# Routing's steps on VectorE with an operand in PSUM, prefix sums by scans, |q| from the bank, and a new order, in an attention and mixture-of-experts layer

## The chip, the cores and the metric

The kernel runs on one NeuronCore of a Trainium2 chip. The metric is the device time of one execution in microseconds (us), as the median of several. TensorE is called PE in the profile (PEld is its weight loads), VectorE is DVE, ScalarE ACT, GpSimd POOL, and SyncE, which issues most DMAs, SP.

## What is computed

The input is x, 4 sequences of 1024 tokens with 128 channels. It is normalised, and two branches are added to x:

```python
xn = layernorm(x)
out = x + attention(xn) + experts(xn)

# attention: 16 heads of 8 channels
q, k, v = heads(xn @ W_attn + b_attn)
s = q @ k.T;  s = s - s.mean(-1)
s = s / (abs(s).mean(-1) + 1e-6) * score_gain        # over all keys
r = max(where(causal, s, -1000), 0) ** 4
y = (r / (r.sum(-1) + 1e-6)) @ v;  return y @ W_proj + b_proj

# experts: 8 experts, each token goes to its best 2
logits = xn @ gate_w + gate_b
topv, topi = top_k(logits, 2);  probs = softmax(topv)
for e in range(8):
    h = (xn @ w1[e] + b1[e]) * (xn @ w2[e] + b2[e])
    y = silu(h @ wg[e] + bg[e]) @ w3[e] + b3[e]
    out += sum(probs * (topi == e)) * y
```

All arithmetic is in float32.

## The kernel before

**The order is a planner's.** The kernel first records nodes: each has a name, a cost for each engine that may do it, what it depends on, the buffers it takes and gives back, and a rank. `Plan.run` then goes through them as a list scheduler: of the nodes that are ready, it takes the one with the earliest start by its own costs, less a bonus `SOONER` for the name (and the name with an engine), and, where starts are equal, the lowest rank plus `RANK` for the name. So two tables of numbers and the costs decide both the order and which engine does a step that can go to more than one (relu on ScalarE or VectorE, squares on ScalarE or GpSimd, sums of |s| on VectorE or ScalarE). The order on each engine is then fixed in the program: every engine works through its own list, strictly in order, and waits by semaphores for the others.

**Start** (to about 35 us). Four `norm` calls make normalised tokens in `blk` buffers (130 columns a token: 128 channels, a column for a gate's weight, a column for a row number), transpose them (`xT`), and compute the gate's logits into `lg` (L529). `prepare(0)` makes keys, queries and values of the first sequence: k and q matmuls (L794), evacuations from the PSUM bank on ScalarE (L802, L806), |q| by ScalarE from the evacuated q (L832), a tiny constant added to it on VectorE (L836), a matmul with the mean |k| (L855) that bounds |s|, and a scaling of q by a power of two that comes from the bound's exponent bits (L841, L844). `blocks` (L885 to L890) forms running sums of k over blocks of 128 keys, and `heads` (L926, L932) uses them. For the other sequences this is done later, between attention work.

**Routing** (`route`) is the mixture's bookkeeping, with the token on the partition and 32 blocks of 128 tokens by 8 experts, 256 elements, on the free axis. All its scratch lies in three SBUF buffers of kind `u`:

- `top` (L586 to L594) finds the best and the second expert by max, compare, multiply by a preference and compare again, and writes two 0/1 arrays `hot` and their sum.
- `counts` (L604, L605) multiplies that sum by a triangle of ones and by ones, so that each token gets its rank within its block and each block its totals.
- `places` (L613 to L619) makes prefix sums over the 32 blocks by six doubling steps of a copy and an add. `tiles_of` (L627 to L644) counts how many tiles of 256 slots each expert needs and sums these over the experts by three doubling steps.
- `slots_of` (L650 to L658), once for each of the two choices, gives each token the row in the scatter buffer `xs`. `owners` (L663 to L671) says which expert each of the 39 tiles belongs to; `bias` (L683) gathers the biases of the tiles' experts by six matmuls.
- `weights` (L700 to L709) makes the two softmax weights from an exp on ScalarE (L599) and fills `we`, which is needed for the bias b3 in the output projection.

Then 64 indirect DMAs on GpSimd's queue scatter 128 rows each to `xs` (L747), each after the one before has landed. The rows' weight column is set to the first weight by `weights` (L704) and to the second by GpSimd (L732) before the second half.

**Attention** is worked in eight chunks (four sequences, two halves of 512 queries), and each chunk in four groups of four heads. `up` (L971) computes all scores of a query block for the sum of |s|, which VectorE (L984) or ScalarE (L986) takes from the bank. `score` (L1095) computes the causal ones transposed; a mask with max (VectorE, L1114) and relu (ScalarE L1121 or VectorE L1123) bring them to SBUF buffers `u1`, two squarings (ScalarE L1146 or GpSimd L1148) to buffers `u`, and `av` (L1171, with L1162 for the sum of the relus) multiplies by the values. Transposes (L1039), a normalisation on VectorE and ScalarE (L1048 to L1060), and the output projection (L1212 to L1237) end a chunk.

**Experts** run beside attention from 290 us on: 39 tiles of 256 slots. For each, SP loads the rows and the expert's weights, PE transposes and does three matrix products (L1276, L1286, L1293, L1302), and GpSimd adds the rows to a DRAM accumulator `acc` by two indirect DMAs (`give`, L1322). At the end `collect` reloads the accumulator in four DMAs (L1410), adds it to the output (L1419), and eight DMAs store it (L1424).

Of the kernel before, what the change touches and what calls it, by code (L numbers as in the profile page):

```python
# [9 lines left out]
I32 = mybir.dt.int32  # L10
U32 = mybir.dt.uint32
AF = mybir.ActivationFunctionType
ALU = mybir.AluOpType
# [3 lines left out]
P = 128  # L17
# [34 lines left out]
class Plan:  # L52
# [6 lines left out]
    SOONER = {"score": 0.67, "mask": -0.22, "norm": -0.9, "tbias": -0.55, "count": 0.79, "rows": 0.11, "v": -0.28, "top": 1.05, "wT": 0.08, "kappa": 0.16, "gateT": 0.62, "k": 0.33, "abs": -0.58, "ys": 0.25, "stats": -0.21, "exp": -0.3, "sq": -0.97, "bound": 0.23, "proj": -0.33, "scale": -0.84, "least": 1.02, "xg": 0.24, "give": 0.78, "bias": 0.7, "yT": -0.13, "std": 0.01, "turn": 0.11, "sum": -0.3, "sums": -0.07, "heads": -0.18, "gate": -0.46, "headsT": -0.01, "normal": -0.04, "load": -0.33, "second": -0.2, "h": 0.16, "relu": -0.23, "keys": -0.53, "y@DVE": -1.2, "gate@DVE": -0.05, "relu@DVE": -0.49, "xT": 0.31, "q@DVE": -0.03, "xg@DVE": -0.53, "yT@ACT": -0.29, "relu@ACT": -0.03, "abs@ACT": 0.05, "out": -1.18, "yT@DVE": 0.3, "xT@DVE": -0.72, "norm@DVE": 0.4, "place": -0.51, "gate@ACT": 0.54, "g": 0.1, "wT@ACT": -0.22, "y@ACT": -0.99, "heads@DVE": -0.21, "fill": 0.06, "heads@ACT": 0.29, "mean": 0.04, "y": 0.98, "abs@DVE": 0.31, "ys@DVE": -0.24, "sq@ACT": 0.32, "warm": 0.42, "xg@ACT": -0.73, "norm@ACT": 0.74, "up": 0.2, "q": 0.22}  # L59
    RANK = {"score": 14, "proj": -177, "yT": 11, "k": -27, "xg": -79, "sums": -3, "h": 8, "sq": 29, "reload": 126, "tbias": -22, "normal": -23, "bound": 51, "top": -177, "headsT": 9, "weight": 88, "spill": -20, "blocks": 6, "place": -4, "sum": -25, "kappa": -91, "std": 28, "gateT": -159, "count": 17, "scatter": 175, "xT": -7, "heads": 20, "y": 3, "exp": -5, "second": -240, "load": 6, "relu": 124, "keys": -42, "mask": -227, "rows": -24, "scale": 209, "out": 16, "turn": -13, "wT": 13, "fill": 16, "ys": -33, "av": -7, "bias": 7, "gain": -11, "g": 186, "q": -113, "give": -27, "gate": -124, "absq": 32, "norm": 26, "warm": 17}  # L60
# [105 lines left out]
def layer_kernel(  # L166
# [152 lines left out]
    for i in range(kinds["V"][0]):  # L319
# [9 lines left out]
    ahead = keep([P, P], "ahead")  # L329
    nc.gpsimd.memset(ahead, 1.0)  # L330
    nc.gpsimd.affine_select(
        out=ahead, in_=ahead, compare_op=ALU.is_gt, fill=0.0,
        base=0, pattern=[[1, P]], channel_multiplier=-1,
# [4 lines left out]
    steps = keep([P, NT // TS], "steps")  # L338
    tiles_f = keep([P, N_TILES], "tiles_f")
    expert_f = keep([P, 1], "expert_f")  # L340
    for t, pattern, base, cm in (
        (first, [[-1, E]], E, 0), (steps, [[TS, NT // TS]], 0, 0),
        (tiles_f, [[1, N_TILES]], 0, 0), (expert_f, [[0, 1]], 0, 1),
    ):
        nc.gpsimd.iota(t, pattern=pattern, base=base, channel_multiplier=cm, allow_small_or_imprecise_dtypes=True)
# [70 lines left out]
    slot = [keep([P, NTB], f"slot_{k}", I32) for k in range(2)]  # L416
    whole = [keep([P, NTB], f"whole_{k}", I32) for k in range(2)]
    owner = keep([P, N_TILES], "owner", I32)
    biases = keep([P, 3, FB, N_TILES], "biases")
    lg = keep([P, NTB, E], "lg")  # L420
# [30 lines left out]
    def norm(b, rank, begin):  # L451
# [66 lines left out]
        def gate(e):  # L518
            for g in range(CB):
# [10 lines left out]
                    lg[:, b * TB : (b + 1) * TB, :], of_buf(k2)[:, : TB * 32].rearrange("p (n e) -> p n e", e=32)[:, :, :E],  # L530
# [12 lines left out]
    grid = [P, NTB, E]  # L543
    over = lambda t: t.unsqueeze(2).to_broadcast(grid)
    flat = lambda t: t.rearrange("p n e -> p (n e)")

    def route(rank):

        bufs = [Buf("u") for _ in range(3)]
        NE = NTB * E  # L550

        def space():

            at = [0] * len(bufs)

            def take(n, shape):
                i = next(i for i in range(len(bufs)) if at[i] + n <= 2 * CH)
                t = of_buf(bufs[i]).rearrange("p k n -> p (k n)")[:, at[i] : at[i] + n]
                at[i] += n
                names = "abc"[: len(shape)]  # L560
                if len(shape) == 1:
                    return t
                kw = {names[i]: shape[i] for i in range(1, len(shape))}
                return t.rearrange(f"p ({' '.join(names)}) -> p {' '.join(names)}", **kw)

            return take

        v = {}

        def top(e):  # L570
            take = space()
            hot, best = [], []
            v["hot"], v["best"] = hot, best
            for k in range(2):
                hot.append(take(NE, (NTB, E)))
            v["sum"] = [take((NTB + 1) * E, (NTB + 1, E)) for _ in range(2)]
            v["both"] = take(NE, (NTB, E))
            v["at"] = [take(NE, (NTB, E)) for _ in range(2)]
            v["small"] = [take(NTB, (NTB,)) for _ in range(8)]
            v["over"] = take(E * (NT // TS), (E, NT // TS))  # L580
            v["past"] = take(N_TILES * E, (N_TILES, E))
            v["ends"] = [take(E, (E,)) for _ in range(4)]
            v["own"] = [take(N_TILES, (N_TILES,)) for _ in range(2)]
            for k in range(2):
                b, m, o = v["small"][k], v["small"][2], hot[k]
                nc.vector.tensor_reduce(b, lg, AX.X, ALU.max)  # L586
                nc.vector.tensor_tensor(o, lg, over(b), ALU.is_equal)
                nc.vector.tensor_tensor(o, o, first.unsqueeze(1).to_broadcast(grid), ALU.mult)
                nc.vector.tensor_reduce(m, o, AX.X, ALU.max)
                nc.vector.tensor_tensor(o, o, over(m), ALU.is_equal)  # L590
                if k == 0:
                    nc.vector.scalar_tensor_tensor(flat(lg), flat(o), -3.0e38, flat(lg), ALU.mult, ALU.add)
            nc.vector.tensor_tensor(v["both"], hot[0], hot[1], ALU.add)
            nc.vector.tensor_tensor(v["small"][3], v["small"][1], v["small"][0], ALU.subtract)  # L594

        n = add("top", {"DVE": 5.0}, top, deps=gated, take=bufs, rank=rank)
        ex = add(
            "exp", {"ACT": 1.5},
            lambda e: nc.scalar.activation(v["small"][3], v["small"][3], AF.Exp), deps=[n], rank=rank,  # L599
        )  # L600
        k1, k2 = Buf("bank"), Buf("bank")

        def counts(e):
            nc.tensor.matmul(of_buf(k1)[:, :NE], ahead, flat(v["both"]), start=True, stop=True)  # L604
            nc.tensor.matmul(of_buf(k1)[:, NE : 2 * NE], ones, flat(v["both"]), start=True, stop=True)  # L605

        m = add("count", {"PE": 1.2}, counts, deps=[n], take=[k1], rank=rank)

        def places(e):

            sums = v["sum"]
            pn = of_buf(k1)
            nc.vector.memset(sums[0][:, 0:1, :], 0.0)  # L613
            nc.vector.tensor_copy(flat(sums[0][:, 1:, :]), pn[:, NE : 2 * NE])
            step = 1
            while step <= NTB:
                a, o = sums
                nc.vector.tensor_copy(o[:, :step, :], a[:, :step, :])
                nc.vector.tensor_tensor(o[:, step:, :], a[:, step:, :], a[:, : NTB + 1 - step, :], ALU.add)  # L619
                sums.reverse()  # L620
                step *= 2

        def tiles_of(e):
            sums = v["sum"]
            before = sums[0]
            full = NT // TS
            nc.vector.tensor_tensor(  # L627
                v["over"], before[:, NTB, :].unsqueeze(2).to_broadcast([P, E, full]),
                steps.unsqueeze(1).to_broadcast([P, E, full]), ALU.is_gt,
            )  # L630
            e0, e1, own, start = v["ends"]
            nc.vector.tensor_reduce(own, v["over"], AX.X, ALU.add)
            nc.vector.tensor_copy(e0, own)
            ends = [e0, e1]
            step = 1
            while step < E:
                a, o = ends
                nc.vector.tensor_copy(o[:, :step], a[:, :step])
                nc.vector.tensor_tensor(o[:, step:], a[:, step:], a[:, : E - step], ALU.add)
                ends.reverse()  # L640
                step *= 2
            v["end"] = ends[0]
            nc.vector.tensor_tensor(start, ends[0], own, ALU.subtract)
            nc.vector.tensor_scalar_mul(start, start, float(TS))  # L644

        def slots_of(e, k):
            hot, (at0, at1), start = v["hot"], v["at"], v["ends"][3]
            pn, before = of_buf(k1), v["sum"][0]
            if k == 0:
# [838 lines left out]
```

## Time and profile before

| | us |
|---|---|
| median of the runs (3) | 940.21 |
| lowest and highest | 939.61, 943.67 |
| the profiled execution | 942.54 |
| its span, first to last instruction | 940.6 |
| busy: PE, ACT, POOL, DVE | 896.6, 794.1, 702.2, 603.7 |
| mean granted PE clock | 0.98 |
| GpSimd's squares L1148, 289 of them | 532.1 |
| routing's scatter DMAs L747, 64 of them | 64.3, the first at 80.9, the last at 280.9 |

A row of the profile names a line of the kernel, the engine, the operation, the buffers (out <- in), the shape, the number of instructions, and for groups the busy time, the mean of one in ns, and the engine's idle time just ahead of them with what ended it. The chain of work that ended last is made up of PE for 76%, POOL for 8%, DVE for 7%. The granted clock is the share of full speed that TensorE was given; a busy time at half clock is twice as long for the same work.

### The profile page before, as it was taken

To read this page: it belongs to the slowest core of one execution; us is meant where nothing else is said; L and a number is where in the kernel's file an instruction comes from. 1 tells how busy PE (TensorE), PEld (TensorE's weight loads), DVE (VectorE), ACT (ScalarE), POOL (GpSimd) and SP (SyncE) were. 2 spreads that over 40 slices of the span, in tenths; PEclk is the share of its full clock that TensorE was granted. 3 is DMA by queue.
4 is the path that set the end of the run, shared out by engine and by line. 5 is a ranking of instruction groups with operands and counts; after the bars stand their busy time and mean duration, and the time that the engine had idled before them with its cause. 6 is when DMAs were issued, how large, how long until landed. Compare 5 with 4: busy or idle time off the path is not lost.

```text
span 940.6 us, 20648 instructions
## 1 busy us (share of the span) xinstructions
PE 896.6 (95%) x7507; PEld 455.6 (48%) x7507; DVE 603.7 (64%) x1541; ACT 794.1 (84%) x1783; POOL 702.2 (75%) x477
## 2 busy tenths in 40 slices
PE   6588999999999999999999999999999999999995
PEld 3335543433345454544465655444456555444443
DVE  7988775566776555555676665555568667555565
ACT  5867899999898789898887988889897889878991
POOL 4454588998986699798665758979866568699990
PEclk9877999999999999999999999999999999999999
DMA  4730000000003222222232222322322223222005
GB/s 106 292 113 13 21 21 24 24 21 21 24 22 105 54 67 56 67 57 76 59 71 62 59 61 58 67 59 69 71 68 55 58 57 63 58 57 57 13 9 182
DMA packets 66274, 58.62 MB, mean 62 GB/s; under 512 B 6463, under 2 KB 62206, under 8 KB 66174
## 3 DMA queue, kind: packets, MB, share of 16 engines
q1 hardware_dynamic: 52168, 47.67, 16.7%
q0 software_dynamic: 13280, 9.38, 7.3%
q8 instruction: 59, 0.97, 0.4%
q10 hardware_dynamic: 726, 0.27, 0.2%
q14 instruction: 41, 0.34, 0.1%
HBM read 36.90 MB, written 20.40 MB: 61 GB/s over the span
## 4 chain that ended last, share of the span: by engine, by line
PE 76%; POOL 8%; DVE 7%; ACT 3%; DMA 2%; issue 2%; ACTq 0%; SPq 0%; POOLq 0%; DVEq 0%
PE bank L971 15%; PE bank L1095 14%; PE bank L1171 13%; PE bank L1162 9%; PE bank L1293 7%; PE bank L1286 7%; POOL u L1148 5%; PE bank L1302 4%; POOL xs L747 3%; PE bank L1039 2%; DVE u L1114 1%; PE bank L1276 1%; DMA blk<-acc 1%; DMA xs<-blk,slot 1%; ACT u L1121 1%
## 5 line engine op out<-in xcount | busy, mean ns | idle before, releaser
L1148 POOL TENSOR_TENSOR u<-u 128x1024 f32<-128x1024 f32 (+1 forms) x289 | 532.1, 1939 | 118.9 <-ACT u L1121 91.3
L1146 ACT ACTIVATE u<-u 128x1024 f32<-128x1024 f32 (+1 forms) x351 | 329.1, 966 | 11.9 <-POOL u L1148 6.1
L984 DVE TENSOR_REDUCE asum<-bank 128x1 f32<-128x512 f32 (+3 forms) x436 | 214.0, 545 | 84.1 <-PE bank L971 82.6
L1121 ACT ACTIVATE u<-bank 128x256 f32<-128x256 f32 (+2 forms) x412 | 178.0, 506 | 49.1 <-DVE u L1114 32.3
L971 PE MATMUL bank<-blk,blk 32*128 32x512 f32 (+3 forms) x1536 | 188.0, 533 | 0.6 <-ACT bank L986 0.4
L1095 PE MATMUL bank<-blk,blk 32*128 32x512 f32 (+3 forms) x1536 | 179.1, 525 | 4.3 <-ACT u L1121 3.1
L986 ACT ACTIVATE bank<-bank 128x512 f32<-128x512 f32 (+3 forms) x332 | 162.4, 491 | 23.2 <-PE bank L971 20.8
L1322 POOL DMA_INDIRECT acc<-ye,xg x78 | 123.3, 1580 | 70.3 <-DVE ye L1314 33.3
L1114 DVE SCALAR_TENSOR_TENSOR u<-bank,causal 128x256 f32<-128x256 f32 (+1 forms) x384 | 121.1, 372 | 79.7 <-PE bank L1095 64.9
L1171 PE MATMUL bank<-u,V 128*32 128x512 f32 (+3 forms) x1536 | 164.5, 501 | 3.6 <-POOL u L1148 3.0
L1162 PE MATMUL bank<-u,pick 128*32 128x512 f32 (+3 forms) x1280 | 128.4, 468 | 0.0
L971 PEld LDWEIGHTS bank<-blk,blk 32*128 32x128 f32 x1536 | 88.5, 187 | 82.2 <-issue 18.0
L1095 PEld LDWEIGHTS bank<-blk,blk 32*128 32x128 f32 x1536 | 66.7, 184 | 71.9 <-issue 23.6
L1123 DVE TENSOR_SCALAR u<-bank 128x512 f32<-128x512 f32 (+1 forms) x100 | 65.2, 673 | 43.5 <-PE bank L1095 42.3
L747 POOL DMA_INDIRECT xs<-blk,slot x64 | 64.3, 1004 | 27.4 <-DMA xs<-blk,slot 16.5
L1162 PEld LDWEIGHTS bank<-u,pick 128*32 128x32 f32 x1280 | 43.5, 111 | 80.7 <-issue 76.4
L1171 PEld LDWEIGHTS bank<-u,V 128*32 128x32 f32 x1536 | 33.8, 108 | 89.0 <-issue 61.5
L1293 PE MATMUL bank<-z,w 128*128 128x256 f32 x312 | 76.8, 389 | 0.0
L1286 PE MATMUL bank<-xT,w 128*128 128x256 f32 x312 | 73.9, 380 | 0.4 <-ACT xT L427 0.4
L1293 PEld LDWEIGHTS bank<-z,w 128*128 128x128 f32 x312 | 56.2, 190 | 27.2 <-issue 11.1
L1368 DVE SCALAR_TENSOR_TENSOR z<-bank,biases,z 128x256 f32<-128x256 f32 x78 | 37.6, 482 | 44.8 <-ACT z L1360 35.7
L986 ACT ACTIVATION_READ_ACCUMULATOR bank<-bank 128x1 f32 x332 | 65.2, 196 | 0.0
(184 smaller groups left out, 720.8 us busy)
## 6 DMA issues: line engine op xcount, KB each, us to landing
w<-in_L_ffn_w_dram SPq DMA_DIRECT2D x117, 128.0 KB
w<-in_L_ffn_wg_dram SPq DMA_DIRECT2D x39, 256.0 KB
xs<-w SPq DMA_DIRECT2D x1, 5070.0 KB
xg<-xs SPq DMA_DIRECT2D x39, 130.0 KB
acc<-w SPq DMA_DIRECT2D x1, 2048.0 KB
blk<-acc SPq DMA_DIRECT2D x4, 512.0 KB
out_dram<-xt SPq DMA_DIRECT2D x8, 256.0 KB
xt<-in_L_attn_x_dram SPq DMA_DIRECT2D x3, 512.0 KB
```

The source lines that it names most:

```text
L971: nc.tensor.matmul(of_buf(ks_[g])[:, at : at + w], of_buf(q[b])[rows_, ii * P : (ii + 1) * P], of_buf(km[b][r])[rows_, k0 : k0 + w], start ...
L984: nc.vector.tensor_reduce(to, of_, AX.X, ALU.add, apply_absolute_value=True)
L986: nc.scalar.activation(of_, of_, AF.Abs, accum_out=to)
L1095: nc.tensor.matmul(of_buf(ks_[g])[:, at : at + n], of_buf(km[b][r])[rows_, jj * P : (jj + 1) * P], of_buf(q[b])[rows_, c * CH + off : (c + ...
L1114: nc.vector.scalar_tensor_tensor(of_buf(u1)[:, g, :near], of_buf(k)[:, :near], 0.0, allowed[:, :near], ALU.max, ALU.mult)
L1121: nc.scalar.activation(to, s_, AF.Relu)
L1146: nc.scalar.activation(to, s_, AF.Square)
L1148: (nc.vector if e == "DVE" else nc.gpsimd).tensor_tensor(to, s_, s_, ALU.mult)
L1162: nc.tensor.matmul(of_buf(acc)[32 * g : 32 * g + 32, off + lo : CH], pick, of_buf(u1s[g // 2])[:, g % 2, at + lo : at + n], start=begin, s ...
L1171: nc.tensor.matmul(of_buf(acc)[32 * g : 32 * g + 32, off:CH], of_buf(Vb[b])[:, jj, h0 : h0 + 32], of_buf(us[g // 2])[:, g % 2, at : at + n ...
L1286: nc.tensor.matmul(of_buf(k)[:, j * TS : (j + 1) * TS], wt[:, f * P : (f + 1) * P], of_buf(tile_[i]["xT"]), start=True, stop=True)
L1293: nc.tensor.matmul(of_buf(k)[:, g * TS : (g + 1) * TS], weights_of(i)[2][:, f, g * P : (g + 1) * P], of_buf(tile_[i]["z"])[:, f, :], start ...
```

## The change

1. **Routing's layout and places.** `lg` and the `hot` arrays are stored expert by expert (8 by 32) instead of token block by token block. `hot`, the weights `pr` and `own` have SBUF tiles of their own; most of the rest lies in two PSUM banks (`k0`, `k1`) and one `u` buffer instead of three. Steps that read or wrote SBUF alone now have an operand, an output or both in a bank.
2. **Prefix sums.** The six doubling steps over the blocks are one `tensor_tensor_scan` over 256 elements that restarts at each expert (`goes_on` is 0 at its first block). The tile counts come from a rounding by a large constant, the sums over experts from a second scan. The ranks within a block come from a matrix of -1 at and above the diagonal, so that inclusive sums become exclusive ones; the sum of the two `hot` arrays is formed in PSUM by two matmuls each, four in place of two.
3. **Fewer instructions.** Rows are computed once for both choices (64 columns). `owners` compares with seven experts.
4. **ScalarE** copies the first `hot` array from its bank and adds 1 to the exp.
5. **Gates.** The three passes that fill `we` go to GpSimd, ahead of the scatters, and the weight column is set there for both choices (eight small copies instead of four on VectorE and four on GpSimd).
6. **|q|** is taken by ScalarE from the bank, beside the evacuation of q. The added constant is gone; instead the mask of the exponent bits is one bit shorter (`-0x1000000`). The bank is given back when both have read it.
7. **Blocks** work in the bank that `heads` uses later; two small instructions are gone.
8. **Plan.** `SOONER` and `RANK` have new values throughout, `give` is planned at 1.9 us instead of 1.2, and the changed steps have new costs. With that, all engines' orders differ from the start, and so does the division: GpSimd does 324 squares (289 before) and ScalarE 316 (351), VectorE 500 sums of |s| (433) and 157 relus (100), ScalarE 268 sums (332) and 355 relus (412).

```diff
+        k0, k1, k2 = Buf("bank"), Buf("bank"), Buf("bank")
+        tmp = Buf("u")
+        room = lambda a, b: of_buf(tmp).rearrange("p k n -> p (k n)")[:, a:b]
+        small = lambda i: of_buf(k0)[:, NE + i * NTB : NE + (i + 1) * NTB]
+        marks = lambda: of_buf(k0)[:, :NE].rearrange("p (e n) -> p e n", e=E)
+        def best(e, k):
+            nc.vector.tensor_reduce(small(k), by_token(lg), AX.X, ALU.max)
+            nc.vector.tensor_tensor(marks(), lg, over(small(k)), ALU.is_equal)
+        def only(e, k):
+            nc.vector.tensor_tensor(marks(), marks(), first.unsqueeze(2).to_broadcast(grid), ALU.mult)
+            nc.vector.tensor_reduce(pr[:, 3, :], by_token(marks()), AX.X, ALU.max)
+            nc.vector.tensor_tensor(marks() if k == 0 else hot[1], marks(), over(pr[:, 3, :]), ALU.is_equal)
...
-            nc.tensor.matmul(of_buf(k1)[:, :NE], ahead, flat(v["both"]), start=True, stop=True)
-            nc.tensor.matmul(of_buf(k1)[:, NE : 2 * NE], ones, flat(v["both"]), start=True, stop=True)
+            for k in range(2):
+                nc.tensor.matmul(of_buf(k1)[:, NE : 2 * NE], ones, flat(hot[k]), start=k == 0, stop=k == 1)
+            for k in range(2):
+                nc.tensor.matmul(of_buf(k1)[:, :NE], behind_, flat(hot[k]), start=k == 0, stop=k == 1)
...
-            nc.vector.tensor_copy(flat(sums[0][:, 1:, :]), pn[:, NE : 2 * NE])
-            while step <= NTB:
-                a, o = sums
-                nc.vector.tensor_copy(o[:, :step, :], a[:, :step, :])
-                nc.vector.tensor_tensor(o[:, step:, :], a[:, step:, :], a[:, : NTB + 1 - step, :], ALU.add)
+            nc.vector.tensor_tensor_scan(upto(), flat(goes_on), of_buf(k1)[:, NE : 2 * NE], 0.0, ALU.mult, ALU.add)
+            nc.vector.tensor_scalar(ends(0), last, 1.0 / TS, 0.5 - 0.5 / TS, ALU.mult, ALU.add)
+            nc.vector.tensor_scalar(ends(0), ends(0), 12582912.0, 12582912.0, ALU.add, ALU.subtract)
+            nc.vector.tensor_tensor_scan(ends(1)[:, 1:], one8[:, : E - 1], ends(0)[:, : E - 1], 0.0, ALU.mult, ALU.add)
...
+        def gates(e):
+            for k in range(2):
+                nc.gpsimd.tensor_tensor(hot[k], hot[k], over(pr[:, 1 + k, :]), ALU.mult)
+            nc.gpsimd.tensor_tensor(we[:, :, :E], by_token(hot[0]), by_token(hot[1]), ALU.add)
...
-            nc.scalar.activation(of_buf(aq)[:, here], of_buf(qb)[:, here], AF.Abs)
-            nc.vector.tensor_scalar_add(t, t, TINY)
+                        nc.scalar.activation(of_buf(aq)[:, here], of_buf(k), AF.Abs, bias=bq)
...
-                        "give", {"POOL": 1.2}, give, deps=[m] + stored[-1:], give=[ye, xg] if j == SB - 1 else [],
+                        "give", {"POOL": 1.9}, give, deps=[m] + stored[-1:], give=[ye, xg] if j == SB - 1 else [],
```

## The prediction

> **What bounds the kernel now.** I read the page's totals, then a table of stretches, since the total hides where TensorE is short of work.
>
> ```profile
> span 940.6 us, 20648 instructions
> PE 896.6 (95%) x7507; PEld 455.6 (48%) x7507; DVE 603.7 (64%) x1541; ACT 794.1 (84%) x1783; POOL 702.2 (75%) x477
> ```
>
> TensorE is the bound over the whole. The stretches (columns: length, busy time of PE, PEld, DVE, ACT, POOL, granted clock, DMA share, GB/s) say where it is not:
>
> ```profile
> 20.00:40.00 20.00, 15.20 (x106) 8.45 (x106) 18.71 (x64) 18.97 (x43) 4.81 (x3) 0.97 0.53 203
> 40.00:60.00 20.00, 12.53 (x122) 5.75 (x122) 18.29 (x43) 11.52 (x26) 10.41 (x7) 0.69 0.76 272
> 60.00:80.00 20.00, 14.58 (x120) 6.97 (x116) 18.59 (x49) 15.16 (x39) 11.36 (x8) 0.82 0.00 1
> 80.00:100.00 20.00, 18.53 (x128) 11.02 (x128) 13.71 (x34) 12.34 (x31) 8.62 (x8) 0.67 0.06 21
> 400.00:500.00 100.00, 99.50 (x836) 53.81 (x836) 62.55 (x155) 86.66 (x190) 75.16 (x45) 1.00 0.29 65
> ```
>
> Between 40 and 80 us VectorE is busy 36.9 of 40 us, TensorE 27.1, and the clock is low. From 100 to 900 TensorE idles some 7 us in all (100 minus its busy time, row by row), so a faster VectorE is worth nothing there. TensorE's own timeline, with the idle time before a row and its releaser in brackets, shows the three holes:
>
> ```profile
> 47.47 1.19 PE L604 MATMUL bank<-u,ahead 128*128 128x256 f32 x2 [9.31 <-DVE u L594]
> 63.31 1.52 PE L1095 MATMUL bank<-blk,blk 32*128 32x256 f32 x3 [2.94 <-ACT u L1121]
> 81.47 2.56 PE L683 MATMUL bank<-u,bes 8*128 8x39 f32 x11 [3.33 <-DVE u L1114]
> ```
>
> The first is the count matmul, which stands in TensorE's order and waits for the top-2 step. In the second ScalarE's relu waited for masks that were queued on VectorE behind routing's copies. The third is the bias matmul, which waits for the owners (L663 to L671, done at 81.1). All three are routing on VectorE. Two-microsecond stretches show a clock of 0.50 from 38.7 to 53.2, 62.7 to 69.3 and 79.8 to 93.3: after each hole TensorE works for 5.7, 4.9 and 11.8 us at half speed, which costs half of that, 11.2 us. Why routing is slow is seen in the order of time on VectorE, with GpSimd's squares above:
>
> ```profile
> 35.19 10.02 POOL L1148 TENSOR_TENSOR u<-u 128x1024 f32<-128x1024 f32 x5 [22.85 <-ACT u L1121]
> 64.81 5.10 POOL L1148 TENSOR_TENSOR u<-u 128x1024 f32<-128x1024 f32 x3 [2.81 <-DVE u L1114]
> ```
> ```profile
> 37.47 1.93 DVE L588 TENSOR_TENSOR u<-u,first 128x256 f32<-128x256 f32 x1
> 45.52 0.42 DVE L588 TENSOR_TENSOR u<-u,first 128x256 f32<-128x256 f32 x1
> 58.38 1.81 DVE L638 COPY u<-u 128x2 f32<-128x2 f32 x1
> 64.78 1.41 DVE L1114 SCALAR_TENSOR_TENSOR u<-bank,causal 128x256 f32<-128x256 f32 x4
> 67.02 2.00 DVE L652 TENSOR_TENSOR u<-u,u 128x256 f32<-128x256 f32 x1
> 71.86 0.41 DVE L652 TENSOR_TENSOR u<-u,u 128x256 f32<-128x256 f32 x1
> ```
>
> The same instruction takes 0.42 us when GpSimd stands still (45.52) and 1.93 inside a square (37.47); a copy of two columns takes 1.81. L1114, with one operand in a bank, runs at 0.35 each inside the squares of 64.81.
>
> **Routing's steps on VectorE.** Before, from the timeline by function: top 10.8, places 5.2, tiles_of 5.2, slots_of 6.5, weights 2.6, owners 4.0: 34.4 us. What exceeds the quick form of the same row (1.51 on L588, 1.56 on L592, 3.25 on the two L638, 1.58 on L652, 1.38 on L663, and so on) sums to 15.1.
>
> After: top is two rounds of five passes over 256 elements at 0.41 (L650, a bank and SBUF: 0.412) to 0.42 (L589, a reduce), one STT of 0.44 and two small copies of 0.18: 4.9. The prefix sums become one scan of 256 elements and one of 7. The only scan in the trace has 8 elements (L889, 0.18); for 256 I bound it by a pass (0.42) and by the slow L588 (1.93) and take 0.55, near the pass; with four small ones places cost 1.1. Slots 0.85, slots_at 1.7, rows once over 64 columns 0.8, owners 1.3, weights 0.7. Sum 11.4. The reduces now read with a stride of 32 elements; no row near shows that at this size; between nothing [...] and double it is 0 to 1.7 us for the four of them, and I take 0.
>
> The Trainium skill speaks against this step: "Perfetto Trace Analysis", section "Optimizing Scalar/DVE Operations", gives VectorE about 60 ns of access overhead on SBUF and 125 on PSUM. By it some 30 instructions would add 2 us, 13.4 in all. The trace has L650 with a bank at 0.412 and L707 without at 0.418, so I stay at 11.4. VectorE saves 23 us.
>
> **What of it reaches TensorE.** In the changed order the bias matmuls stand behind nearly the same TensorE work (score 7.0 against 7.5 units of four 512-column matmuls, up 3 against 4, av and pick alike): 1.5 units less, at 1.07 us (tail rows of L971) 1.6 us that comes back later. Between the first mask (33.9 before) and the owners, VectorE's changed list has 28 masks (0.28 to 0.41 each) and one relu, 9.9 us, blocks 1.9, seven abs at 0.68, 4.8, the gate rows and a shead copy 0.7, and 10.7 of routing: some 28 us, where before it needed 47. The first mask comes about a microsecond later (14 norm pieces of 0.28 on VectorE instead of 8, two copies of 0.35 more, two L836 of 0.43 less), so the owners could be done at 63. Two other engines are next: ScalarE has 24 us of relus, squares, abs and an exp table load after its keys end near 37, 61 at the earliest; GpSimd has ten large squares of 1.9 and five of 1.04 from 36 on, 60. Three full engines chained to each other don't run without waits; I allow 5.5 us and put the bias matmul at 68.5 instead of 81.5: **-13.0**.
>
> The clock: "TensorE: Matmul & The Clock Gate", section "Part 1: The HAM clock gate", says that the clock falls after an idle window of about 3.4 us and that shorter gaps keep it. By that nearly all 11.2 us return, as no step left is 3 us long. The trace is stricter: a gap of 2.94 us brought 0.50. TensorE still starves before 68 us, where a slow clock is covered by the wait; only the burst behind it (84 to 93, 5.9 us lost now) counts, and I give it half: **-3.0**.
>
> Costs: units that move behind +1.6; four count matmuls instead of two, 0.55 each (half of L604's 1.19 and L605's 1.06, which ran at half speed), +1.1. These are TensorE's own.
>
> **Off the path.** |q| from the bank takes the eight L836 (3.7 us) from VectorE and makes ScalarE's pass 0.69 instead of 0.63 (L806 against L832); the bank is held until both readers are done, 0.7 us, while eight banks are there; blocks lose L886 and L888 (0.8 us in all). Three of four batches do this at full TensorE: nothing. If the cover went it would be 1 us. Gates on GpSimd: three passes over 256 elements, by L1148's 1.04 at 512 about 0.6 each, 2 us, and four more copies of 0.2 stand ahead of or between scatters; the first scatter waits 2 us longer, but starts some 10 us sooner, and the experts follow near 277 instead of 290. That alone saves nothing: TensorE has attention work meanwhile.
>
> **The replanned order.** GpSimd gets 324 squares instead of 289 (65 small instead of 50), VectorE 67 more abs rows and 57 more relus, ScalarE loses 64 abs, 57 relus, 35 squares. Give is planned at 1.9 us instead of 1.2; a give and the square behind it take 3.67 us in the trace (599.55 to 603.22), less 1.9 for the square is 1.77, so the plan is nearer now. Where TensorE is full this can gain at most the 7 us of idle and cost what GpSimd delays; I take +1.0. In the tail, the last chunk's normalisation no longer stands behind the sum of a reload (L1048 ran at 927.35 though its transposes ended at 924.99: -2.4), but the last give is now behind the last small square (919.36 to 920.4; the give went at 915.46 before), which starts the reloads up to 5 us later. Between -2.4 and +3 I take 0.
>
> **Sum.** -13.0 - 3.0 + 1.6 + 1.1 + 1.0 = -12.3. The profiled execution took 942.54 us, 1.94 around its span; less 12.3 it is 930.2. It stood 2.3 above the median of 940.21, so the median should be **928.0**.
>
> **Rivals.** (a) ScalarE and GpSimd take VectorE's place: the bias matmul comes at 75, the clock stays low: -6.5 + 3.7, near 937; with a share of the clock 935. For it: the changed ScalarE list has waits on GpSimd in it. Against: ScalarE was busy 26.7 of 40 us there. Chance 0.15. (b) The plan also removes the idle of 100 to 900 and the 2.4 of the tail: 919. For it ScalarE's relief, as it is at 94% between 100 and 250. Chance 0.15. (c) Slower: GpSimd becomes the bound among the experts. With squares of 1.9 and 1.04 and gives of 1.77, experts 8 to 11, 16 to 19 and 32 to 35 need 63, 62 and 64 us of GpSimd (59 at most before); waits for gives (23.3 and 33.3 us over 78) add 6, for the second of a pair another 6, so 75, while TensorE gives four experts 64. Three stretches at 11 are 33; if neighbours take up a third, +22 - 12 is 950. It decides once TensorE's waits for squares, 16.7 us now, grow by over 12. Against it: squares are spread among eight buffers. Chance 0.10. (d) The bank operand doesn't help, rows stay at 1.5 to 2 us: of the 23 us, 15 go, and what is left is shared with ScalarE's limit: 937. L1114 speaks against it. Chance 0.08. The forecast has 0.52.
>
> **Chances.** A measurement of this kernel tells 0.5%, 4.7 us, from no change. Faster: forecast, (b) and half of (a), 0.76; same: the rest of (a) and most of (d), 0.13; slower 0.11. The range goes from (b) with its own spread, 916, to (a) and (d), 938; (c) is left out.
>
> **What would show it.** No routing row on VectorE over 0.6 us; the bias matmuls before 72; TensorE idle under 10 us between 40 and 80 (12.9 now); clock above 0.85 from 80 to 100. Wrong if TensorE waits for squares among the experts, or the reloads land after the last projection.

## The result and the profile after

| | before | after |
|---|---|---|
| median of 19 runs | 940.21 (937.46 to 943.77) | 933.04 (930.50 to 939.14) |
| ratio | | 0.9927, 95% interval 0.9910 to 0.9944 |
| profiled execution, span | 942.54, 940.6 | 934.0, 932.3 |

The change gains 0.7% (some 7 us), where 12.3 were forecast. The page's totals after:

```profile
span 932.3 us, 20608 instructions
PE 901.4 (97%) x7517; PEld 458.4 (49%) x7517; DVE 644.5 (69%) x1616; ACT 718.1 (77%) x1564; POOL 756.1 (81%) x519
```

The view by stretches, with columns as before:

```profile
40.00:60.00 20.00, 19.94 (x183) 9.24 (x186) 18.07 (x51) 16.89 (x33) 15.99 (x11) 0.98 0.61 214
...
80.00:100.00 20.00, 20.00 (x188) 10.55 (x188) 16.58 (x41) 16.76 (x46) 15.80 (x14) 1.00 0.07 25
220.00:240.00 20.00, 15.99 (x108) 6.08 (x100) 16.89 (x22) 11.20 (x16) 18.30 (x14) 0.83 0.08 25
...
460.00:480.00 20.00, 15.03 (x97) 6.70 (x99) 15.24 (x24) 10.84 (x19) 11.79 (x8) 0.83 0.20 42
```

The starved region of before is gone: from 40 to 100 us TensorE idles 0.3 us at a clock of 0.98 to 1.00. But two rows further on show what before did not have: 4 to 5 us of idle and a low clock at 220 and at 460 us. TensorE's timeline has no hole before the bias matmul, which comes 17.4 us earlier than before:

```profile
64.11 1.38 PE L664 MATMUL bank<-own,bes 8*128 8x39 f32 x11
```

**A table of lost time.** For each kernel I cut the profiled execution into 2-us stretches and summed TensorE's idle time and its busy time multiplied by one minus the granted clock.

| lost, us | before 100 us | 100 to 880 | after 880 | all |
|---|---|---|---|---|
| before | 38.6 | 6.9 | 10.4 | 55.9 |
| after | 11.9 | 21.7 | 8.4 | 42.0 |

The last stretch, shorter than 2 us, is left out. By the table 26.7 us were won early and 14.8 lost again in the middle. Span less loss is 884.7 and 890.3; for the twelve kernels below it lies between 886.8 and 892.6. So a sum of losses can be off by some 5 us, and before's stands out most: from before to after the loss falls by 13.9 us, the span by 8.3. Why isn't shown; the low clock alone isn't the reason, since kernel 6 below lost more to it (15.1 us against 12.6) and has 891.1.

**Where the middle's loss is.** The stretch from 220 to 240 holds 7.1 us of it, 280 to 300 4.3, 460 to 480 8.1. The first and the last are where the second and third sequences' keys and queries are prepared. VectorE's, GpSimd's and TensorE's timelines there:

```profile
222.69 2.51 DVE L797 TENSOR_TENSOR cstat<-cstat 128x1 f32<-128x1 f32 x1
...
226.08 2.74 DVE L816 TENSOR_TENSOR blk<-blk,blk 128x512 f32<-128x512 f32 x1
...
229.45 2.73 DVE L816 TENSOR_TENSOR blk<-blk,blk 128x512 f32<-128x512 f32 x1
...
457.49 1.21 DVE L803 TENSOR_REDUCE cstat<-blk 128x1 f32<-128x1024 f32 x1
...
458.92 2.82 DVE L805 TENSOR_SCALAR kapB<-same,cstat,sign 128x128 f32<-128x128 f32 x1
...
463.75 4.17 DVE L816 TENSOR_TENSOR blk<-blk,blk 128x512 f32<-128x512 f32 x1
...
468.95 0.69 DVE L816 TENSOR_TENSOR blk<-blk,blk 128x512 f32<-128x512 f32 x1
```
```profile
449.96 11.69 POOL L1119 TENSOR_TENSOR u<-u 128x1024 f32<-128x1024 f32 x6
...
463.75 3.62 POOL L1119 TENSOR_TENSOR u<-u 128x512 f32<-128x512 f32 x3
```
```profile
228.97 1.63 PE L942 MATMUL bank<-blk,blk 32*128 32x512 f32 x4 [1.33 <-DVE blk L816]
...
461.89 1.95 PE L825 MATMUL bank<-blk,kapB 128*128 128x512 f32 x4 [1.63 <-DVE cstat L797]
...
468.07 2.38 PE L942 MATMUL bank<-blk,blk 32*128 32x512 f32 x8 [3.33 <-DVE blk L816]
```

L816, the product that scales q, takes 0.69 us at 468.95 and 4.17 at 463.75, from the start of GpSimd's three squares to half a microsecond past their end. L805 takes 2.82, from inside the last but one of a run of six squares to the end of the run. L803, a reduction inside the same run, takes its usual 1.21. It is the stretching that slowed routing before, now in `prepare`. In before these rows had the same operands but other neighbours: L844 (now L816) took 0.79 us on average, L826 (now L805) 0.35. VectorE's and GpSimd's timelines of before at the third sequence show it: GpSimd stood still for 7.58 us there.

```profile
469.65 0.69 DVE L844 TENSOR_TENSOR blk<-blk,blk 128x512 f32<-128x512 f32 x1
```
```profile
474.32 1.89 POOL L1148 TENSOR_TENSOR u<-u 128x1024 f32<-128x1024 f32 x1 [7.58 <-ACT u L1121]
```

The new order put GpSimd's squares beside these rows.

### The profile page after: what moved, and what is told of

It is laid out like the page before. It is cut to its first block, busy times and chain, and to the rows that moved or that the text cites. A ratio compares the mean times of both kernels' runs of the same rounds, so it can differ in the third digit from the quotient of the medians.

```text
span 932.3 us, 20608 instructions
## 1 busy us (share of the span) xinstructions
PE 901.4 (97%) x7517; PEld 458.4 (49%) x7517; DVE 644.5 (69%) x1616; ACT 718.1 (77%) x1564; POOL 756.1 (81%) x519
## 4 chain that ended last, share of the span: by engine, by line
PE 83%; DVE 7%; POOL 6%; issue 2%; DMA 1%; ACT 1%; SPq 0%; ACTq 0%; POOLq 0%; DVEq 0%
PE bank L942 17%; PE bank L1066 16%; PE bank L1142 14%; PE bank L1133 9%; PE bank L1264 8%; PE bank L1257 7%; PE bank L1273 4%; POOL u L1119 4%; PE bank L1010 2%; POOL xs L723 1%; PE bank L767 1%; PE bank L1247 1%; DVE blk L816 1%; PE bank L1426 1%; DMA blk<-acc 1%
## 5 line engine op out<-in xcount | busy, mean ns | idle before, releaser
L1119 POOL TENSOR_TENSOR u<-u 128x1024 f32<-128x1024 f32 (+1 forms) x324 | 582.1, 1924 | 99.4 <-ACT u L1092 62.7
L1117 ACT ACTIVATE u<-u 128x1024 f32<-128x1024 f32 (+1 forms) x316 | 298.2, 971 | 11.7 <-POOL u L1119 5.6
L955 DVE TENSOR_REDUCE asum<-bank 128x1 f32<-128x512 f32 (+3 forms) x500 | 243.0, 543 | 62.1 <-PE bank L942 61.3
L1092 ACT ACTIVATE u<-bank 128x256 f32<-128x256 f32 (+2 forms) x355 | 152.4, 492 | 71.9 <-DVE u L1085 44.0
L942 PE MATMUL bank<-blk,blk 32*128 32x512 f32 (+3 forms) x1536 | 188.4, 529 | 7.1 <-DVE blk L816 4.7
L1085 DVE SCALAR_TENSOR_TENSOR u<-bank,causal 128x256 f32<-128x256 f32 (+1 forms) x384 | 121.2, 372 | 89.6 <-PE bank L1066 70.9
L957 ACT ACTIVATE bank<-bank 128x512 f32<-128x512 f32 (+3 forms) x268 | 130.5, 488 | 35.1 <-PE bank L942 31.8
L1094 DVE TENSOR_SCALAR u<-bank 128x512 f32<-128x512 f32 (+2 forms) x157 | 98.9, 656 | 55.9 <-PE bank L1066 55.9
L942 PEld LDWEIGHTS bank<-blk,blk 32*128 32x128 f32 x1536 | 90.6, 185 | 86.1 <-issue 13.5
L723 POOL DMA_INDIRECT xs<-blk,slot x64 | 64.5, 1008 | 21.4 <-DMA xs<-blk,slot 11.2
L1257 PEld LDWEIGHTS bank<-xT,w 128*128 128x128 f32 x312 | 56.9, 193 | 7.7 <-DVE asum L955 1.5
L1339 DVE SCALAR_TENSOR_TENSOR z<-bank,biases,z 128x256 f32<-128x256 f32 x78 | 37.2, 478 | 30.8 <-ACT z L1331 30.7
```

Of the source, the lines that this page charges most:

```text
L942: nc.tensor.matmul(of_buf(ks_[g])[:, at : at + w], of_buf(q[b])[rows_, ii * P : (ii + 1) * P], of_buf(km[b][r])[rows_, k0 : k0 + w], start ...
L955: nc.vector.tensor_reduce(to, of_, AX.X, ALU.add, apply_absolute_value=True)
L957: nc.scalar.activation(of_, of_, AF.Abs, accum_out=to)
L1092: nc.scalar.activation(to, s_, AF.Relu)
L1117: nc.scalar.activation(to, s_, AF.Square)
L1119: (nc.vector if e == "DVE" else nc.gpsimd).tensor_tensor(to, s_, s_, ALU.mult)
```

## The experiments

Changes in us below are the ratio to before less one, times 940.2, so that kernels timed on different chips compare. "Old tables" are `SOONER` and `RANK` of before with give at 1.2 us.

| kernel | median | ratio (95%) | change | lost: before 100, to 880, after |
|---|---|---|---|---|
| after | 933.04 | 0.9927 (0.9910 to 0.9944) | -6.9 | 11.9, 21.7, 8.4 |
| 1 product from the bank | 925.42 | 0.9857 (0.9831 to 0.9883) | -13.4 | 15.2, 7.1, 8.3 |
| 2 and kapB, column sum | 923.22 | 0.9831 (0.9805 to 0.9857) | -15.9 | 19.0, 8.3, 7.8 |
| 3 routing in SBUF | 939.47 | 1.0010 (0.9995 to 1.0025) | +0.9 | 18.9, 17.1, 8.8 |
| 4 old tables | 920.26 | 0.9804 (0.9778 to 0.9830) | -18.4 | 14.2, 5.0, 7.5 |
| 5 old tables, edit 2 | 929.42 | 0.9880 (0.9854 to 0.9906) | -11.3 | 21.3, 10.6, 7.5 |
| 6 new tables, old code | 965.38 | 1.0281 (1.0257 to 1.0304) | +26.4 | 38.5, 11.2, 21.3 |
| 7 old tables, edit 3 | 931.78 | 0.9907 (0.9884 to 0.9930) | -8.7 | 21.8, 8.3, 9.8 |
| 8 routing alone, old tables | 937.74 | 0.9979 (0.9966 to 0.9992) | -2.0 | 15.9, 17.8, 7.3 |
| 9 edit 2, sequences 1 to 3 | 920.50 | 0.9793 (0.9769 to 0.9817) | -19.5 | 20.2, 6.3, 7.6 |
| 10 old tables, edit 9 | 924.78 | 0.9830 (0.9804 to 0.9855) | -16.0 | 14.7, 11.2, 7.6 |
| 11 old tables, old \|q\| | 922.92 | 0.9829 (0.9799 to 0.9860) | -16.1 | 15.0, 7.8, 7.9 |
| 12 old tables, gates on VectorE | 924.33 | 0.9831 (0.9807 to 0.9856) | -15.9 | 17.2, 6.9, 9.0 |

**1. The product from the bank.**

```diff
+            nc.vector.tensor_scalar(
+                bound.bitcast(I32), bound.bitcast(I32), 0x7F800000, -0x1000000, ALU.bitwise_xor, ALU.bitwise_and
+            )
-            nc.vector.tensor_tensor(of_buf(qb)[:, here], of_buf(qb)[:, here], t, ALU.mult)
+            nc.vector.tensor_tensor(of_buf(qb)[:, here], of_buf(qb)[:, here], bound, ALU.mult)
```

> The changed kernel, with one thing more: the scaling of q is computed a second time, in place in the bank, and the product L816 takes its factor from the bank instead of from SBUF (one VectorE pass of 0.68 us more per half, eight in all; order of all engines otherwise the same). Theory 1 (the late stalls come from VectorE instructions of the next sequence's preparation, with SBUF operands only, which stand still while GpSimd squares): the product takes 0.7 us everywhere (2.7, 2.7 and 4.2 us in the changed kernel), TensorE's wait for it before the next sequence's score sums (4.7 us) falls under 1.5, the granted clock stays up after it, and the time falls by 5 to 9 us against the changed kernel, to 924 to 928. Theory 2 (the new order itself places the preparation too late; the long product is only where it shows): the waits stay, the extra passes cost, 932 to 935. Theory 3 (GpSimd's larger load holds the experts back): no effect, 933.

Measured: 6.5 us faster than the changed kernel. VectorE's timeline, where GpSimd again runs three squares from 457.43 to 461.05:

```profile
452.60 2.83 DVE L805 TENSOR_SCALAR kapB<-same,cstat,sign 128x128 f32<-128x128 f32 x1
...
457.31 0.69 DVE L816 TENSOR_SCALAR bank<-bank 128x512 int32<-128x512 int32 x1
458.04 0.69 DVE L819 TENSOR_TENSOR blk<-blk,bank 128x512 f32<-128x512 f32 x1
```
```profile
458.87 1.43 PE L945 MATMUL bank<-blk,blk 32*128 32x512 f32 x8 [0.45 <-DVE blk L819]
```

Though VectorE does one pass more, TensorE waits 0.45 instead of 3.33 us, and all eight products take 0.686 to 0.689. L805, left as it was, still takes 2.83. Theories 2 and 3 said no change or slower: they fall for this part.

**2. kapB and the column sum too.**

```diff
-            nc.vector.tensor_tensor(mean, ks[:, 0:1], ks[:, 1:2], ALU.add)
+            nc.vector.tensor_scalar(mean, ks[:, 0:1], ks[:, 1:2], None, ALU.add)
-            nc.vector.tensor_scalar(kapB[b % 2], same, kab, sign, ALU.mult, ALU.mult)
+            nc.vector.tensor_scalar(kab, kab, sign, None, ALU.mult)
+            nc.scalar.activation(kapB[b % 2], same, AF.Identity, scale=kab)
```

> As the kernel with the product from the bank, and besides the sum of two columns L797 is a tensor_scalar with one SBUF operand and the 128x128 matrix kapB (L805) is made by ScalarE instead of VectorE (one small VectorE product with the sign more). Theory 1: the remaining long rows of the preparation (2.5 us for the column sum, 2.8 us for kapB) go too, the three waits of TensorE for the bound matmul (3.0 us) fall under 1, and the time is 917 to 923, 10 to 16 below the changed kernel. Theory 2: 931 to 935, with the same waits put down to other rows. Theory 3: 933.

Measured: 9.0 us below the changed kernel, 923.2, at the edge of what theory 1 gave; the intervals don't tell it from kernel 1. The bound matmul's waits for kapB and the column sum fall from 3.0 to 1.5 us, not under 1, and its weight loads wait 2.9 us for kapB instead of 1.6. The early loss rose to 19.0: in the first sequence ScalarE waits 1.5 us for kapB's factor with its masked keys behind it, which start at 30.8 instead of 28.8 us. Kernel 9 tests that.

**3. Routing's scratch in SBUF**, the same instructions in the same order:

```diff
-        small = lambda i: of_buf(k0)[:, NE + i * NTB : NE + (i + 1) * NTB]
-        marks = lambda: of_buf(k0)[:, :NE].rearrange("p (e n) -> p e n", e=E)
+        s0 = s1 = keep([P, 368], "s0")
+        small = lambda i: s0[:, NE + i * NTB : NE + (i + 1) * NTB]
+        marks = lambda: s0[:, :NE].rearrange("p (e n) -> p e n", e=E)
-        ends = lambda i: of_buf(k1)[:, NE + i * E : NE + (i + 1) * E]
+        ends = lambda i: s1[:, NE + i * E : NE + (i + 1) * E]
```

> The changed kernel with routing's scratch in one SBUF tile instead of the two banks (the count matmuls' results are still read from their bank); same instructions, same order on all engines. Theory that the bank operand gives the early gain: the rows that now have SBUF operands only are stretched to 1.5 to 2.5 us where GpSimd squares, routing takes 8 to 15 us longer, the bias matmul comes at 72 to 80 instead of 64, the clock falls after the holes, and the time is 8 to 18 us above the changed kernel, 941 to 951, or less where the later stalls take it up. Rival (fewer instructions and the new order give it): rows of 0.4 to 0.7 us, bias matmul before 67, 932 to 936.

Measured: 7.8 us above the changed kernel, at the level of before. VectorE's timeline:

```profile
42.08 1.78 DVE L573 TENSOR_TENSOR s<-s,first 128x256 f32<-128x256 f32 x1
...
47.23 0.41 DVE L573 TENSOR_TENSOR s<-s,first 128x256 f32<-128x256 f32 x1
...
58.62 1.82 DVE L616 TENSOR_SCALAR s<-s 128x8 f32<-128x8 f32 x1
```

The stretched rows are back and the bias matmul comes at 70.9 instead of 64.1. It was expected at 72 to 80: several rows of routing fall where GpSimd stands still. The early loss is 7 us higher, but 5 of that is the clock, and kernels 1, 2 and 9, with the scratch in the bank, lost 15 to 20 us there too; so it is the medians that put 7.8 us (give or take 2) on the bank operand. What else makes up the early gain, fewer instructions or other places, was not measured apart; kernel 4 shows that it isn't the new tables.

**4 and 6. The tables exchanged.** Only the two lines of tables and the cost of `give` differ.

> The changed kernel's code with the tables SOONER and RANK of before and give planned at 1.2 us again. Theory 1: the early gain is the code's, so TensorE's loss before 100 us stays within 5 us of the changed kernel's (12 us of idle and half clock, 39 before); whether the preparation's SBUF rows meet squares depends on the order, so the late stalls can be gone (then 920 to 926) or others come. Theory that the order gives the early gain: loss before 100 us over 25 us, bias matmul after 74, time 935 to 945.

> The code of before under the new tables and give at 1.9 us. Theory A (the new order costs some 13 us, whatever the code): 948 to 956. Theory B (the new tables suit the new code and are neutral or better without it): 935 to 941. Theory C (tables tuned for one set of nodes fit no other, either way): worse than before by more than the 13, over 956, with new waits at other places.

Kernel 4 is 11.6 us faster than the changed kernel (by the ratios, give or take 3), with the bias matmul at 64.2 all the same. The early gain is the code's; the new tables cost 11.6. Kernel 6 is 26 us slower than before, twice what theory A gave, as theory C had it: the early loss is that of before, 4 us are new in the middle and 11 in the tail. GpSimd's timeline there:

```profile
939.37 1.57 POOL L1322 DMA_INDIRECT acc<-ye,xg  x1 [3.62 <-ACT ye L1317]
943.36 1.57 POOL L1322 DMA_INDIRECT acc<-ye,xg  x1 [2.42 <-DMA acc<-ye,xg]
```

The last gives come one after another behind GpSimd's last square (which ends at 930.4), each waiting for its rows or for the give before it, and the reloads, issued at 946.7, wait for the last of them. These tables did not suit the nodes of before.

**5 and 10. Edit 2 under the old tables**, in all sequences, and only in sequences 1 to 3.

> The changed code under the old tables (920.3), and in it the preparation's rows freed from SBUF-only operands as before (scaling's factor from the bank, the column sum with one operand, kapB on ScalarE). Theory 1 (these rows cost only where the order lays them beside GpSimd squares): under the old tables TensorE waits for them 1.6 us in all, so at most 1 to 2 us are gained, and eight passes of 0.68 us more on VectorE may cost as much: 918 to 922. Rival (the preparation is a bottleneck in any order): 912 to 916.

> The same edit, for sequences 1 to 3 only, under the old tables, where the edit in all four sequences took 929.4 and no edit 920.3. Theory 1: the 9 us lost came from the first sequence's preparation alone, so 917 to 920. Rival (the extra passes on VectorE and kapB on ScalarE hurt at each change of sequence under this order): 923 to 929.

Kernel 5 is 7.1 us slower than kernel 4, against both expectations; in the profiled execution 7.1 us more are lost at the start (3.9 of it idle time, the rest the clock), where ScalarE waits 2.5 us for kapB's factor at 20.55, and 5.6 in the middle. Without the first sequence's part (kernel 10) the start is as in kernel 4. Its 924.8 lies in the rival's range, but by the ratios it is within 2.4 us of kernel 4, which the intervals don't tell apart; in the profiled execution the middle lost 6 us more. Where the order lays few squares beside `prepare`, the edit gains nothing.

**7. Routing in SBUF under the old tables.**

> The changed code under the old tables (920.3), with routing's scratch in SBUF instead of the banks. Theory: the bank operand is worth what the same edit showed under the new tables, 6.4 us, so 925 to 929, with the bias matmul 4 to 8 us later than 64.2 and a part of TensorE's loss of before back between 60 and 80 us. Rival (the loss depends on where squares fall, and under the old tables GpSimd has fewer of them early): 920 to 923.

9.7 us slower than kernel 4, more than the 6 to 7 expected; the bias matmul comes at 73.3, and the early loss is up by 7.6 (2.8 of it idle time). The bank operand is worth 8 to 10 us under either tables.

**8. Routing alone.** The code of before with `route` and what belongs to it as changed, `prepare` as before.

> The code of before with routing, counts, gates and places as changed, but |q|, the added constant and the blocks as before, under the old tables. Theory: routing is all of the gain and the change of |q| and blocks lies off the path, so 918 to 923 (the changed code under the old tables took 920.3). Rival (fewer VectorE and ScalarE steps ahead of the first mask are a part of it): 924 to 930.

Both expectations missed: 937.7. The early gain is there (bias matmul at 64.2, 15.9 lost), so routing alone makes it; but the middle loses 17.8. One stall of it, on GpSimd, VectorE and TensorE:

```profile
447.43 10.99 POOL L1122 TENSOR_TENSOR u<-u 128x1024 f32<-128x1024 f32 x7
```
```profile
454.08 4.63 DVE L810 TENSOR_SCALAR blk<-blk 128x512 f32<-128x512 f32 x1 [1.86 <-ACT blk L806]
...
460.06 0.35 DVE L800 TENSOR_SCALAR kapB<-same,cstat,sign 128x128 f32<-128x128 f32 x1
```
```profile
460.46 3.56 PE L829 MATMUL bank<-blk,kapB 128*128 128x512 f32 x4 [4.05 <-DVE kapB L800]
```

L810 adds the tiny constant to |q|, 0.42 us when alone. Here it stands until the seven squares are over, kapB queues behind it, and TensorE waits 4.05 us. It is the instruction that the change removes as part of |q|. The same tables gave this code a different order from kernel 4's, since the nodes differ.

**9. Edit 2 without the first sequence, under the new tables.**

> The changed kernel under its own tables; the preparation's rows are freed from SBUF-only operands (factor from the bank, column sum with one operand, kapB on ScalarE) for sequences 1 to 3 only, and the first sequence's is left as it was. With the edit in all four, kapB on ScalarE held the masked keys back by 2 us at the start and TensorE's loss before 100 us was 19 instead of 12 us. Theory 1 (the late stalls are the lock of these rows, and the first sequence's edit cost what it seems): loss before 100 us back at 12, 916 to 919. Rival (the order of the new tables costs some 10 us in other ways): 923 to 926.

920.5, between the two ranges: 12.6 us below the changed kernel, so that all that the new tables cost is regained by three edits in `prepare`. The middle's loss is 6.3. The start, which is now the changed kernel's instruction by instruction, lost 20.2 all the same, but TensorE's idle time in it is the changed kernel's, 10.2 us: the 8 us more are the clock (see the end). In kernel 2 it was 10.7. So the early part of kernel 2's loss was put down to kapB too readily.

**11 and 12. The parts off the path**, undone in kernel 4's own order.

> The changed code under the old tables (920.3), with |q| taken from the evacuated q in SBUF again, the added constant on VectorE and the old mask; routing and blocks as changed, all orders kept, with the eight additions in the place of |q|. Theory that it lies off the path except at the start: 920 to 923, the loss before 100 us up by 1 to 2. Rival (it stands in the chain to the next sequence's scores and shows there): 924 to 930 with waits of TensorE for the bound or the scaled q.

> The changed code under the old tables (920.3), with the three passes that fill the gates' weights on VectorE instead of GpSimd, at the same place in the order. Theory (gates are off the path wherever they are, but on VectorE they have SBUF operands only and can stand still for up to 2 us each beside a square): 920 to 924, a few us of VectorE in rows of up to 2 us near 66 us. Rival (GpSimd's 2.5 us ahead of the first scatter matter): 916 to 919.

Both come out 2.3 to 2.5 us slower than kernel 4, with intervals that overlap: neither is told from nothing. The three passes for the gates took 0.42, 0.42 and 0.66 us on VectorE, not the 2 us that a square beside them would have made of them.

No kernel beats 4 and 9, which are level at -2.0%.

## Why the prediction held in sign and missed in size

928.0 was forecast, 933.04 measured, inside the range. Two terms were off, in opposite directions: the code's gain was 5 us larger than the forecast, the order's cost over 10 us. That the sum came as near as it did is in part luck.

- **What of routing reaches TensorE: -13.0 and -3.0 were too little.** The owners were ready at 64.0; my count gave 63 at the earliest, and the 5.5 us that I allowed for waits among three full engines were 1. The bias matmul moved by 17.4. No hole was left, so the clock came back whole: 5.9 us in the burst from 80 to 100, where I gave 3.0. Measured with the old tables, all but the new order is worth -18.4 (interval -20.9 to -16.0), where my terms without the order sum to -13.3. That kernel's order isn't quite that of before either, as its nodes differ. In the clock's sum the second hole was misread: TensorE worked 6.0 us at half speed after it, not 4.9, and the burst's 5.9 us belong to 81.5 to 93, not 84 to 93. The forecast rests on the 5.9 alone, so neither changes it.
- **Routing on VectorE: 11.4 forecast, 12.6 measured** (the rows in order of time). The four strided reductions took 0.61 to 0.63 us and not 0.42; I took 0 of a range of 0 to 1.7. The long scan took 0.68, I took 0.55. So of the signs that I had named, the limit of 0.6 us for a routing row was passed, narrowly; the bias matmul, the idle time and the clock came out as said. Rows with a bank operand took 0.41 to 0.43 inside squares, as the row of L650 said.

```profile
40.42 0.62 DVE L568 TENSOR_REDUCE bank<-lg 128x32 f32<-128x256 f32 x1
...
42.21 0.42 DVE L573 TENSOR_REDUCE pr<-bank 128x32 f32<-128x256 f32 x1
...
54.38 0.68 DVE L611 TENSOR_TENSOR_SCAN u<-goes_on,bank 128x256 f32<-128x256 f32 x1
...
57.83 0.42 DVE L629 TENSOR_TENSOR u<-bank,hot 128x256 f32<-128x256 f32 x1
58.29 0.63 DVE L630 TENSOR_REDUCE bank<-u 128x32 f32<-128x256 f32 x1
```

- **The replanned order: +1.0 forecast, +11.6 measured (give or take 3).** This is the term that failed. I argued that at a full TensorE an order can gain at most the 7 us of idle and cost what GpSimd delays, and looked for that cost among the experts. There it isn't: waits for squares fell from 16.7 to 14.3 us, and rival (c) did not happen. It is at the changes of sequence, where GpSimd's squares came to lie on VectorE rows with SBUF operands alone. I had found that mechanism in routing and applied it to routing only. The Trainium skill ("SBUF — State Buffer", "Who interferes with whom") names the kinds that contend: two inputs from SBUF, or copies and tensor_scalar in two-port modes; the list of `prepare`'s rows against it (L797, L805, L816) would have shown the exposed rows before any run. By the same section reductions on this chip never contend, and L803 kept its 1.21 us beside squares. (VectorE got 64 sums of |s| more, 500 against 436 in the trace of before, not 67; ScalarE's busy share from 100 to 250 us was 92%, not 94.)
- **Off the path: 0 was right only in some orders.** In kernel 8 the kept addition to |q| held TensorE for 4.05 us; I had priced a lost cover at 1 us. In kernel 4's order the whole of |q| came to some 2 us, within the noise.
- **The tail: 0 forecast, -2.4 found.** From the end of the last `av` matmul to the end it took 16.96 us before and 14.55 after; L1019 ran at 919.21, right behind the last transposes, which end at 919.12, and the last give went at 913.58, ahead of the attention's end at 917.75. It isn't the new tables' doing: kernel 4's tail lost 7.5 us, against 10.4 before, and so it is part of the -18.4.
- **The first scatter** went at 68.1 instead of 80.9, the experts' first transposes at 280.5 instead of 290 (277 forecast).

The table of lost time shows no other place: early -26.7, middle +14.8, tail -2.0. Which single entries of the tables bring the squares beside `prepare` was not tried; nor is the stall of 280 to 300 traced to one wait (kernels 1, 2 and 9 don't have it).

## What to carry to other kernels

An engine conflict found in one place is a property of instructions, not of that place: list every VectorE instruction, reductions apart, that reads SBUF alone and stands ahead of a matmul, and give each an operand in PSUM, another engine, or a time at which GpSimd stands still. When code and a planner's tables change together, run the new code with the old tables too: here the code was worth 18.4 us and the tables took 11.6 of it back. An order is itself a large term: kernels that differ in a few nodes under the same tables (4 and 8) lie 16 us apart.

## What was not expected of the hardware

- **A VectorE instruction can stand through several GpSimd instructions.** L816 stood through three squares (4.17 us), L810 of kernel 8 until the end of a run of seven (4.63). It isn't always so: in before, L588 at 37.47 met the second of five squares in a row and was done at 39.40, with the run going on to 45.21. In the fourteen traces, where a row of over 1.3 us came through inside a run, the next square's record begins within 0.1 us of the former's end; where it stood on, the two records overlap by some 0.6 us. Why isn't shown. One square is enough for a small row: an addition of one column (L797, 0.15 us alone) took 2.51.
- **A strided reduction is slower from SBUF than from PSUM.** With steps of 32 elements it took 0.62 us from SBUF (L568, L630) and 0.42 from the bank (L573), for the same 256 elements; with the scratch in SBUF (kernel 3) the latter took 0.58 to 0.60.
- **The clock is low for whole steps of 3.41 us, and where the steps fall differs from execution to execution.** By the clock records of the fourteen traces, each of the 47 low stretches that ended within its trace lasted 3.41, 6.83, 10.24 or 13.65 us, and within one trace they begin whole steps apart (in the changed kernel's at 37.4, 231.9 and 279.7, that is 57 and 14 steps). The changed kernel and kernel 9 have the same instructions for their first 220 us, yet before 100 us the first was low once, from 37.4 to 40.8, and the other three times: from 12.3 to 15.7, 36.2 to 46.4 and 66.9 to 73.7. By the view of stretches (clock in the third column from the right), the changed kernel had

```profile
42.00:47.00 5.00, 5.00 (x58) 2.05 (x50) 4.71 (x14) 4.25 (x7) 3.85 (x4) 1.00 1.03 371
```

and in kernel 9

```profile
42.00:47.00 5.00, 5.00 (x31) 1.59 (x34) 4.75 (x13) 3.22 (x5) 3.53 (x3) 0.56 1.03 371
```

A single profiled execution is thus uncertain by several us in its clock term; the medians decide.
- **The clock also fell where TensorE counts as busy.** From 276.81 to 280.53 sixteen L942 matmuls took 3.78 us, against 2.00 for sixteen at 265.92, with no idle time shown; the clock was 0.50 from 279.7 to 286.6. Matmuls' ends are modelled in the profile, so such waits may hide in them; that isn't shown.
